# Values put off by a step, Strassen's form in all but three first layers, gates broadcast by DMA

## The chip, the cores and the metric

The kernel runs on one core of a Trainium2 chip. The metric is the time of one execution on the device in microseconds, the median of four runs. The profile is that of one execution.

## The reference

The input x has 8 images of 256 channels and 32 x 32 pixels (1024 tokens each). All is float32. Two layers follow one another:

- Layer 0: group normalisation; queries by a 1x1 convolution; keys and values by another one, then pooled to four sizes (32, 16, 11 and 5 squared, 1426 places), each with a 3x3 depthwise convolution added and a layer normalisation; attention with 8 heads of 32 channels; a small mixing matrix between channels; a projection, added to x.
- Layer 1, on tokens: layer normalisation, attention with one head of 256 channels over 1024 tokens, added. Then layer normalisation and a mixture of 8 experts, added. The experts are where part of the change lies:

```
feat = mean(x, axis=0);  w = softmax(feat @ Wr + br)      # gates, by token place and expert
h = relu(bn(x @ W1[e] + b1[e]))                           # first layer, 256 -> 256
h = relu(bn(h @ W2[e] + b2[e]))                           # second layer
y = h @ Wo[e] + bo[e]                                     # third layer
out = sum over e of y * w[:, e]
```

The gates depend on the mean over all 8 images, so they are known only when attention of the last image has ended.

## The kernel before

Channels lie on the 128 partitions (two blocks of 128), tokens along the free axis. TensorE, ScalarE (ACT), VectorE (DVE), GpSimd (POOL) and the transfers of SyncE (SP) run at the same time, each through its own queue, in program order. What the program order is, a planner in the kernel decides while the program is built: the class `Flow` keeps a modelled clock for each engine and for each tile the time at which it will be ready or free. Work is written as generators ("threads") that yield what they need next: an engine, tiles, and a PSUM tag. `Flow.step` runs threads that its model finds runnable. Without an argument it is closed for TensorE and lets only the other engines' work through. With a pair of paces it first adds credit, up to 1.5 times the pace, for threads of rank under 5 and for those of rank 5 and above; TensorE's work of a thread is let in while its class has credit, or while TensorE's clock is earlier than the time at which the score buffer will be free. `Flow.finish` runs threads until a condition holds. All instructions pass through line 668, so the profile's groups are told apart by tile names.

*Stage 1, layer 0's attention with layer 1's attention beside it (0 to about 1990 us).* 384 steps: 8 images, 2 groups of 4 heads, 2 halves of 512 queries, 12 chunks of up to 128 keys. In a step four matmuls (`scores`) fill the tile `sc` (128 x 4 x 512, half of PSUM, one buffer), four heads side by side by rows of the array; ACT takes exp of it into `pt` (six buffers). Then four matmuls (`values`) of the chunk before add into `pv` (one buffer, one bank), side by side by columns. Every two chunks POOL issues a DMA that adds the odd chunk's `pt` onto the even one's (`add`); DVE adds these pairs up to the sum for the softmax (`sums`), and a unit of 12 chunks ends with ACT's copy of `pv`. The work of other threads that fills TensorE between these is called filler here: projections, transposes, normalisations, all of layer 1's attention (`layer1`, `outputs`). It goes through the PSUM tags `sm` (two buffers) and `sx` (one).

The order in a step of the loop at the end of `attention` is: scores of chunk i and their exp, a closed step, values of chunk i - 1, the pair's addition, and a step with the paces 4 and 2 us for filler.

*Stage 2, experts beside the end of layer 1 (about 1990 to 2275 us).* A tile is half an image (512 tokens), item i is one expert on one tile, 128 items. While the thread `gates` is not done, the loop runs first and second layers of the items in turn, each of four matmuls of 512 columns (two instructions each), and lets the planner put the rest of layer 1 and the gates between. Second layers' results (`h2`) are stored to DRAM (`h2d`). At its end `gates` broadcasts each gate row to 128 partitions by a matmul with `sel` and an ACT copy into `gates` (16 times), and makes four tiles of the output's bias.

*Stage 3 (to the end).* Pools of layer 1 are closed and new ones opened. First and third layers go in Strassen's form (the Winograd variant): seven matmuls of 256 columns on combinations of the weights (`weights`, on POOL) and of the input (`combined`, on DVE), and `sums` on DVE and ACT to put the seven products of a first layer together (`first7`). Stored results are fetched (`fetch`), multiplied by their gate and combined (`weigh`), and third layers add up over the eight experts in PSUM (`third`).

Of the kernel before, what the change touches and what calls it, by code (L numbers as in the profile page):

```python
# [13 lines left out]
PSUM = bass.MemoryType.PSUM  # L14
# [20 lines left out]
AHEAD = {"DVE": 4.0, "ACT": 2.0, "POOL": 1.0, "SP": 10.0}  # L35
NEAR = {"DVE": 1.5, "ACT": 2.0, "POOL": 1.0, "SP": 10.0}
BUFS = {"sm": 2, "sx": 1}
PACE2 = 8.0
NBOUND = 64
# [840 lines left out]
def attention(tc, kit, f, outer, ended, nb, consts, x, t1, t2, hn, bounds, vecs, q_t, kv_t, proj_t, gqk_t, wqk, wqkv, vecs1, w1_d, w1c, gate_d, wrc, vecs2, bnvec):  # L880
# [6 lines left out]
    with ExitStack() as ctx:  # L887
# [924 lines left out]

        pts = {}
        for i in range(len(steps) + 1):
            if i < len(steps):
                b, c, half, kc = steps[i]
                sl = slice(half * 512, half * 512 + 512)
                if kc % 4 == 0:
                    f.finish(lambda: key_parts[0] > 3 * b + kc // 4)
                if (half, kc) == (0, 0):  # L1820
                    f.finish(lambda: (b, c) in qs and (b or (c, 0) in asked))
                    turn[0] = 2 * b + c
                    atts[b, c] = T(work, [P, HW], "att", bufs=2)
                if i == 4:
                    f.finish(lambda: {0, 1}.issubset(whole))
                if b == 0 and kc == 0:
                    f.finish(lambda: (c, half) in asked)
                pts[i] = scores(b, c, sl, kc)
                f.step()
            if i:  # L1830
                b1, c1, half1, kc1 = steps[i - 1]
                if kc1 == 0:
                    pv = T(psum, [P, 512], "pv")
                    pairs = []
                    sl1 = slice(half1 * 512, half1 * 512 + 512)
                    f.spawn(unit(b1, c1, sl1, i // NKC, pairs), 0)
                f.finish(lambda: kc1 // 4 in vts[b1])
                values(b1, c1, kc1, pts[i - 1], pv)
                if kc1 % 2:
                    add(kc1, pts.pop(i - 1), pts[i - 2])  # L1840
                    pairs.append(pts.pop(i - 2))
                if kc1 == NKC - 1:
                    f.finish(lambda: projected[0] >= b1)
                    f.act.activation(atts[b1, c1][:, sl1], pv, AF.Copy)
            if i < len(steps):
                f.step((PACE, PACE1))
        f.finish(lambda: projected[0] == nb)
# [139 lines left out]

def experts(tc, kit, nb, t2, hn, h2d, w1c, w2_d, wo_d, bnvec, bo_d, gate_d, wrc, consts8, out, f, outer, ended, early):

# [10 lines left out]
    with ExitStack() as ctx:  # L2000
# [24 lines left out]
        f.sp.dma_start(br, gate_d[:, 2 * NE :])  # L2025
        sel = T(wg, [NE, NE * P], "sel")
        f.sp.dma_start(sel, consts8[:, : NE * P])
        bo = T(wg, [NE, C], "bo")
# [3 lines left out]
        gt = T(wg, [NE, HW], "gt")  # L2032
        gb = T(wp, [P, NE, HW], "gates")
        gated = []

        def gates():


# [36 lines left out]
            for half in range(2):  # L2075
# [5 lines left out]
                f.ve.tensor_copy(gt[:, half * 512 : half * 512 + 512], ps[:NE, :])  # L2081
            for half in range(2):
                sl = slice(half * 512, half * 512 + 512)
                for e in range(NE):
                    yield "PE", (gt,), "sm"
                    ps = T(shared, [P, 512], "sm", bufs=2)
                    f.pe.matmul(ps, lhsT=sel[:, e * P : (e + 1) * P], rhs=gt[:, sl], start=True, stop=True)
                    f.act.activation(gb[:, e, sl], ps, AF.Copy)
            added = T(wp, [P, 2, HW], "featsum")
# [42 lines left out]

        def second(i, staged):
            _, e, _, _ = where(i)
            h, src = T(work, [P, 2, 512], "h2", bufs=5), h1s.pop(i)
            for m in range(2):
                half(h, w2[e], e, src, 2, 3, m)
                yield
            if staged:
                f.sp.dma_start(h2d[i], h)  # L2140
            else:
                h2s[i] = h

        def fetch(i):
            if i not in h2s:
                h = h2s[i] = T(work, [P, 2, 512], "h2", bufs=5)
                f.sp.dma_start(h, h2d[i])

        total = 2 * nb * NE
        f.spawn(gates(), 7)  # L2150
        n1 = n2 = n3 = 0

        while not gated and n2 < NSTAGED:
            first(n1)
            n1 += 1
            f.step((PACE2, PACE2))
            if n1 > 1:
                for _ in second(n2, True):
                    pass
                n2 += 1  # L2160
                f.step((PACE2, PACE2))
        f.finish(lambda: gated)
        early.close()
        wp3 = ctx.enter_context(tc.tile_pool(name="w3", bufs=1, side="right"))
        psum_y = ctx.enter_context(tc.tile_pool(name="psum_y", bufs=1, space=PSUM, side="right"))

        def blocks(w):

            return w[:, 0, :P], w[:, 1, :P], w[:, 1, P:]

        def weights(w, tag):
            s = T(wp3, [P, 4, P], tag)
            a11, a12, a22 = blocks(w)
# [5 lines left out]

        def combined(h, tag):  # L2180

            t = T(wp3, [P, 4, C], tag, bufs=2)
            f.ve.tensor_tensor(t[:, 0:2, :], h[:, :, C:], h[:, 0, :].rearrange("p (n q) -> p n q", n=2), ALU.subtract)
            f.ve.tensor_tensor(t[:, 2, :], h[:, 1, C:], t[:, 0, :], ALU.subtract)
            f.ve.tensor_tensor(t[:, 3, :], h[:, 1, :C], t[:, 2, :], ALU.subtract)
            return t
# [22 lines left out]
        def sums(banks):  # L2209

            c = T(wp3, [P, 4, C], "c", bufs=2)
            u = T(wp3, [P, 2, C], "u", bufs=2)
            p26, p57, p34 = (banks[i].rearrange("p (u q) -> p u q", u=2) for i in (0, 2, 3))
            p1 = T(wp3, [P, 1, C], "p1c", bufs=2)
            f.act.activation(p1[:, 0, :], banks[1][:, :C], AF.Copy)
# [6 lines left out]
        def first7(i):  # L2222
# [10 lines left out]
            if e == NE - 2 and tile_i + 1 in xs:  # L2233
                ts[tile_i + 1] = combined(xs[tile_i + 1], "t1")

        def weigh(i):
            _, e, _, sl = where(i)
            h = h2s[i]
            f.ve.tensor_tensor(h, h, gb[:, e : e + 1, sl].to_broadcast([P, 2, 512]), ALU.mult)
            h2s[i] = h, combined(h, "t3")  # L2240

# [14 lines left out]

        s1, s3 = {}, {}
        for i in range(NE):
            s3[i] = weights(wo[i], f"s3e{i}")
            e = (n1 + i) % NE  # L2260
            s1[e] = weights(w1[e], f"s1e{e}")

# [10 lines left out]

        for i in range(2):
            fetch(i)
        weigh(0)
# [19 lines left out]
def tile_conv_attn_hybrid(  # L2296
# [35 lines left out]
    w1c = T(dram, [P, NE, 2, C], "w1c")  # L2332
    wrc = T(dram, [P, 2, NE], "wrc")
    h2d = [T(dram, [P, 2, 512], f"h2_{i}") for i in range(2 * nb * NE)]

# [3 lines left out]
    flag = T(cpool, [P, 1], "flag")  # L2339
    last = partial(experts, tc, kit, nb, t2, hn, h2d, w1c, w2_d, wo_d, bnvec, bo_d, gate_d, wrc, consts8, out)  # L2340
    with ExitStack() as early:
# [132 lines left out]
```

## Time and profile before

| | |
|---|---|
| median of 4 runs (lowest to highest) | 3383.7 us (3379.43 to 3385.47) |
| the profiled execution: time, span | 3385.09 us, 3382.8 us |
| granted TensorE clock, mean | 0.978 |
| TensorE, DVE, ACT, POOL busy | 95%, 67%, 50%, 15% of the span |
| TensorE busy from 0 to 2000 us | 1845 us |
| TensorE busy from 2050 to 2270 us | all of it |

An engine's idle time costs something only where the engine sets the pace. Durations of matmuls are modelled and overlap by their ends, so the distance from one start to the next is the better measure: two instructions of 512 columns start 0.43 us apart, of 256 columns 0.22 us. A matmul in float32 is two instructions. A wait is given as engine and tile that waited, what released it, and the time in total, the number of waits and the longest.

### The profile page before, as it was taken

Reading aid. Unit: us, or ns where it says so; the run is one execution under the profiler, and the core shown is the slowest. Engines: PE = TensorE matmul, PEld = TensorE weight load, DVE = VectorE, ACT = ScalarE, POOL = GpSimd, SP = SyncE. Lnnn points to the kernel's source line nnn. Section 1 sums busy time; section 2 is a strip of 40 time slices with the busy share of each in tenths; the row PEclk is TensorE's granted clock in tenths of the full one; section 3 lists DMA queues with packets and bytes.
Section 4 is the critical chain, followed back from the end, with each engine's and each line's share of the span. In section 5 each row is a group of like instructions: output and inputs, shape, how many; then the busy total and the mean of one; then the engine's idle time right before and its main releaser. Section 6 shows DMA issues by size and latency. Waiting matters only on the chain.

```text
span 3382.8 us, 39921 instructions
## 1 busy us (share of the span) xinstructions
PE 3201.3 (95%) x15270; PEld 1781.6 (53%) x15270; DVE 2266.3 (67%) x3890; ACT 1694.3 (50%) x2222; POOL 519.1 (15%) x644
## 2 busy tenths in 40 slices
PE   8687899899899999899999989999999999999998
PEld 4322245344345345344344446637777777777775
DVE  6687787886986887877875444207766666666665
ACT  4476676576576666666665533342233333333332
POOL 2211414213213214213212110013000000000000
PEclk9798999999999999999999999999999999999999
DMA  2366646646656566556557563213430000000000
GB/s 74 82 128 156 137 93 156 134 98 152 134 127 126 125 149 125 115 129 128 111 118 153 116 204 136 79 72 134 162 106 19 31 26 19 19 19 19 19 13 20
DMA packets 102328, 335.37 MB, mean 99 GB/s; under 512 B 12576, under 2 KB 37928, under 8 KB 78896
## 3 DMA queue, kind: packets, MB, share of 16 engines
q0 software_dynamic: 28608, 179.85, 27.7%
q1 hardware_dynamic: 70160, 150.91, 13.0%
q8 instruction: 122, 2.00, 0.2%
q10 hardware_dynamic: 3360, 1.97, 0.2%
q14 instruction: 78, 0.64, 0.1%
HBM read 97.28 MB, written 70.26 MB: 50 GB/s over the span
## 4 chain that ended last, share of the span: by engine, by line
PE 49%; DVE 1%; ACT 1%; DMA 0%; issue 0%; SPq 0%; DVEq 0%; ACTq 0%
PE bank L668 25%; PE y L668 11%; PE sm L668 7%; PE sc L668 2%; PE sx L668 2%; PE pv L668 2%; ACT pt L668 1%; DVE t L668 0%; DMA h<-h 0%; DMA hn<-hn 0%; DVE h L668 0%; DVE pt L668 0%; DMA t<-pt 0%; DVE rec L668 0%; DVE c L668 0%
## 5 line engine op out<-in xcount | busy, mean ns | idle before, releaser
L668 ACT ACTIVATE pt<-sc 128x2048 f32<-128x2048 f32 (+1 forms) x384 | 719.9, 1875 | 325.7 <-PE sc L668 271.4
L668 DVE SCALAR_TENSOR_TENSOR acc<-p,vec,acc 128x225 f32<-128x225 f32 (+7 forms) x928 | 526.5, 574 | 28.6 <-ACT acc L668 4.1
L668 PE MATMUL sc<-q,kn 32*128 32x512 f32 (+1 forms) x3072 | 448.1, 653 | 93.2 <-ACT pt L668 91.5
L668 DVE TENSOR_TENSOR pt<-pt,pt 128x1024 f32<-128x1024 f32 x320 | 387.3, 1253 | 144.0 <-DMA pt<-pt 134.3
L668 PE MATMUL bank<-h,w2e 128*128 128x512 f32 x1024 | 478.2, 593 | 0.0
L668 ACT ACTIVATE h<-bank,bnvec 128x512 f32<-128x512 f32 x300 | 231.2, 771 | 476.9 <-PE bank L668 456.8
L668 PE MATMUL pv<-pt,vt 128*32 128x512 f32 (+1 forms) x3072 | 422.6, 623 | 0.0
L668 ACT ACTIVATE h<-c,bnvec 128x512 f32<-128x512 f32 x212 | 161.0, 807 | 321.8 <-DVE c L668 321.8
L668 POOL DMA_DIRECT2D pt<-pt x192 | 173.7, 905 | 778.5 <-ACT pt L668 611.3
L668 DVE TENSOR_TENSOR c<-p1c,bank 128x512 f32<-128x512 f32 x106 | 72.8, 687 | 309.2 <-PE bank L668 309.2
L668 PEld LDWEIGHTS bank<-h,w2e 128*128 128x128 f32 x1024 | 193.9, 190 | 151.0 <-issue 139.4
L668 PEld LDWEIGHTS sc<-q,kn 32*128 32x128 f32 (+1 forms) x3072 | 116.6, 179 | 285.4 <-ACT pt L668 185.4
L668 PEld LDWEIGHTS pv<-pt,vt 128*32 128x32 f32 (+1 forms) x3072 | 61.0, 108 | 303.6 <-issue 292.9
L668 POOL TENSOR_TENSOR rstd<-rstd,mhalf 128x4 f32<-128x4 f32 (+2 forms) x88 | 105.7, 1202 | 688.7 <-DVE rstd L668 593.2
L668 DVE TENSOR_TENSOR h<-h,gates 128x1024 f32<-128x1024 f32 x128 | 157.3, 1229 | 71.4 <-DMA h<-h 64.3
L668 PE MATMUL bank<-hn,w1e 128*128 128x256 f32 (+1 forms) x600 | 191.6, 448 | 10.2 <-DMA hn<-hn 10.2
L668 PE MATMUL y<-t,s3e 128*128 128x256 f32 x768 | 188.0, 381 | 0.0
L668 PE MATMUL sm<-y,t 128*128 128x256 f32 x752 | 180.4, 385 | 0.0
L668 PEld LDWEIGHTS sm<-y,t 128*128 128x128 f32 x752 | 137.9, 190 | 56.1 <-issue 34.4
L668 PEld LDWEIGHTS bank<-hn,w1e 128*128 128x128 f32 x600 | 114.4, 192 | 100.2 <-issue 92.7
L668 ACT ACTIVATE p<-sm 128x512 f32<-128x512 f32 (+1 forms) x151 | 88.5, 586 | 146.5 <-PE sm L668 124.6
L668 PE MATMUL bank<-t,s1e 128*128 128x256 f32 x636 | 155.7, 381 | 2.0 <-DVE t L668 2.0
(306 smaller groups left out, 4671.6 us busy)
## 6 DMA issues: line engine op xcount, KB each, us to landing
pt<-pt POOLq DMA_DIRECT2D x160, 1024.0 KB, 7.4
h<-h SPq DMA_DIRECT2D x76, 512.0 KB, 4.2
xi<-in_x_dram SPq DMA_DIRECT2D x16, 512.0 KB, 6.0
t<-t SPq DMA_DIRECT2D x8, 1024.0 KB, 9.3
res<-t SPq DMA_DIRECT2D x32, 256.0 KB, 4.1
t<-res SPq DMA_DIRECT2D x32, 256.0 KB, 5.0
hn<-res SPq DMA_DIRECT2D x32, 256.0 KB, 2.9
hn<-hn SPq DMA_DIRECT2D x16, 512.0 KB, 5.3
```

The costliest lines, as they stand in the source:

```text
L668: ins = fn(*args, **kwargs)
```

## The change

In the attention loop the filler step comes before the values. Values of the chunk before are put off by one step if it is the only one outstanding and the planner's TensorE clock, plus SLACK of 0.5 us, has passed the time at which `sc` will be free. In the next step both chunks' values are issued. After values a step runs with paces of zero, which also cuts the credit that is left over to zero.

In the experts' stage the combined weights of W1 are made by POOL at the start, in the pool where the gates lay; only the first three first layers are plain, all others take `first7`. The thread `gates` writes its 8 x 1024 result to a DRAM tile `gtd`; the 16 sel matmuls and ACT copies go. After the old pools have been closed, 16 DMAs read rows of `gtd` into the 128 partitions of the new tile `gates`, and two more rounds of first and second layer run before the first `weigh`.

```diff
-NEAR = {"DVE": 1.5, "ACT": 2.0, "POOL": 1.0, "SP": 10.0}
+NEAR = {"DVE": 1.5, "ACT": 2.0, "POOL": 1.0, "SP": 1.0}
+SLACK = 0.5
...
                 pts[i] = scores(b, c, sl, kc)
                 f.step()
+            if i < len(steps):
+                f.step((PACE, PACE1))
             if i:
-                b1, c1, half1, kc1 = steps[i - 1]
+                late.append(i - 1)
+            if i < len(steps) and len(late) == 1 and f.now["PE"] + SLACK > f.free("sc"):
+                continue
+            while late:
+                k = late.pop(0)
+                b1, c1, half1, kc1 = steps[k]
...
-                values(b1, c1, kc1, pts[i - 1], pv)
+                values(b1, c1, kc1, pts[k], pv)
                 if kc1 % 2:
-                    add(kc1, pts.pop(i - 1), pts[i - 2])
-                    pairs.append(pts.pop(i - 2))
+                    add(kc1, pts.pop(k), pts[k - 1])
+                    pairs.append(pts.pop(k - 1))
...
             if i < len(steps):
-                f.step((PACE, PACE1))
+                f.step((0, 0))
...
-        sel = T(wg, [NE, NE * P], "sel")
-        f.sp.dma_start(sel, consts8[:, : NE * P])
...
-        gb = T(wp, [P, NE, HW], "gates")
...
-            for half in range(2):
-                sl = slice(half * 512, half * 512 + 512)
-                for e in range(NE):
-                    yield "PE", (gt,), "sm"
-                    ps = T(shared, [P, 512], "sm", bufs=2)
-                    f.pe.matmul(ps, lhsT=sel[:, e * P : (e + 1) * P], rhs=gt[:, sl], start=True, stop=True)
-                    f.act.activation(gb[:, e, sl], ps, AF.Copy)
+            f.sp.dma_start(gtd, gt)
...
+        s1 = {e: weights(w1[e], f"s1e{e}", wp) for e in range(NE)}
+
+        def ahead():
+            nonlocal n1, n2
+
+            (first if n1 < 3 else first7)(n1)
+            if n1 == 0:
+                ts[0] = combined(xs[0], "t1")
+            n1 += 1
+            f.step((PACE2, PACE2))
+            if n1 > 1:
+                for _ in second(n2, True):
+                    pass
+                n2 += 1
+                f.step((PACE2, PACE2))
+
+        f.step((PACE2, PACE2))
+        while not gated and n2 < NSTAGED:
+            ahead()
+        f.finish(lambda: gated)
+        early.close()
+        wp3 = ctx.enter_context(tc.tile_pool(name="w3", bufs=1, side="right"))
+
+        gb = T(wp3, [P, NE, HW], "gates")
+        f.split(gb, *(512 * i for i in range(1, 2 * NE)))
+        for part in range(2):
+            sl = slice(part * 512, part * 512 + 512)
+            for e in range(NE):
+                f.sp.dma_start(gb[:, e, sl], gtd[e : e + 1, sl].to_broadcast([P, 512]))
...
         for i in range(NE):
-            s3[i] = weights(wo[i], f"s3e{i}")
-            e = (n1 + i) % NE
-            s1[e] = weights(w1[e], f"s1e{e}")
+            s3[i] = weights(wo[i], f"s3e{i}", wp3)
...
         for i in range(2):
+            ahead()
             fetch(i)
         weigh(0)
```

The tiles of `combined` and `sums` for first layers move to the pool `work2`; those of third layers stay in `w3`.

## The prediction

> **What bounds the kernel now.** I read the page first, then the waits, then TensorE's timeline at three places, then the chain. The page says that TensorE is busy nearly everywhere:
>
> ```profile
> PE 3201.3 (95%) x15270; PEld 1781.6 (53%) x15270; DVE 2266.3 (67%) x3890; ACT 1694.3 (50%) x2222; POOL 519.1 (15%) x644
> ...
> PE   8687899899899999899999989999999999999998
> ```
>
> So a change is worth what it takes off TensorE's work or idle time, and little else. The third slice (about 85 to 340 us) holds the worst of it; from about 2000 us on only one gap is left. The waits name the idle time:
>
> ```profile
> ACT pt L668 <- PE sc L668: 271.4, 250, 3.9
> ...
> DVE pt L668 <- DMA pt<-pt: 134.3, 59, 8.5
> ...
> PE sc L668 <- ACT pt L668: 91.5, 93, 3.3
> ...
> ACT pt L668 <- DMA pt<-pt: 15.4, 7, 3.5
> ```
>
> The third line is what part one aims at: scores (sc) wait for exp (pt), since sc has one buffer. The fourth is the next limit: exp waits 7 times for a free buffer of pt. Two ways in which a step goes, from the timeline (start, length, instructions, idle time before in brackets):
>
> ```profile
> 893.30 1.14 PE L668 MATMUL sc<-q,kn 32*128 32x512 f32 x8
> 894.37 1.07 PE L668 MATMUL pv<-pt,vt 128*32 128x512 f32 x8
> 896.44 1.14 PE L668 MATMUL sc<-q,kn 32*128 32x512 f32 x8 [1.00 <-ACT pt L668]
> ...
> 1711.28 1.14 PE L668 MATMUL sc<-q,kn 32*128 32x512 f32 x8
> 1712.35 1.06 PE L668 MATMUL pv<-pt,vt 128*32 128x512 f32 x8
> 1713.34 1.99 PE L668 MATMUL sx<-p,v 128*128 128x256 f32 x8
> 1715.27 1.14 PE L668 MATMUL sc<-q,kn 32*128 32x512 f32 x8
> ```
>
> A step without other work lasts 3.14 us, 1.00 of it idle. A full one has scores 1.07, values 0.99 and one filler 1.93, with no wait. The third place is the passage from layer 1 to the last stage:
>
> ```profile
> 2220.83 1.98 PE L668 MATMUL sm<-gt,sel 8*128 8x512 f32 x4
> 2222.74 3.70 PE L668 MATMUL bank<-hn,w1e 128*128 128x512 f32 x8
> 2226.37 1.98 PE L668 MATMUL sm<-gt,sel 8*128 8x512 f32 x4
> ...
> 2272.60 3.70 PE L668 MATMUL bank<-h,w2e 128*128 128x512 f32 x8
> 2284.30 2.04 PE L668 MATMUL y<-h,wo 128*128 128x256 f32 x4 [7.99 <-DVE h L668]
> ```
>
> The gates' broadcast costs TensorE time between expert layers, and the first third layer comes after 7.99 us of idle. Last, the chain, whose pieces give the steady rhythm:
>
> ```profile
> 2334.64 4.74 PE bank L668 x18
> 2347.14 4.74 PE bank L668 x18
> ...
> 2517.38 6.46 PE bank L668 x22
> 2526.86 6.45 PE bank L668 x22
> ```
>
> **The change, part by part**, against the profiled execution: span 3382.8, time 3385.1, which is 1.4 above the median 3383.7.
>
> *First layers.* 300 ACT writes of h from bank by two, less 128 second layers, are 22 plain first layers; 106 are in Strassen's form. After, three stay plain, so 19 change. The rhythm 12.50 holds one third layer more than the rhythm 9.48 (50 instructions against 36), so 14 instructions of 256 columns take 3.02 us. A plain layer takes 3.44 (8 instructions: 2181.52 to 2184.96). 19 x 0.42 = 8 us less on TensorE. Each adds DVE sums (0.69 + 0.69 + 0.42 + 0.68 = 2.5 us) and an ACT copy of 0.38; they lie beside TensorE, in 2000 to 2200 where DVE is 28 to 39% busy. Without this cover they would cost up to 19 x 2.5 = 47 us. All four banks are taken, but second's two are read before the next product needs them: banks 1 and 0 by the sums 0.7 to 2.3 us into the products.
>
> *Weights' sums on POOL.* The 32 for w1 move from 2272 to the start of the stage. At 0.46 us each from the first landing (issued 1994.7, 6.6 to landing) they end at 2016, just when POOL's next work, rstd at 2016.7, stands in the queue behind them. At the contended 0.64 to 1.44 they'd delay layer 1's last norms by about 10 us; TensorE has expert layers to fill that (busy throughout 2050 to 2270). Costed at nothing; if the fill failed, 10 us.
>
> *Gates.* One pair of sel matmuls and the expert half between takes 5.54 us (2220.83 to 2226.37), the half alone 3.44: 2.10 a pair, eight pairs, 17 us less. ACT loses 16 copies of 0.60, off the path. Added: one write of gt and 16 loads of 256 KB on SP. The eight loads of wo took SP 4.92 us, so 16 take 9.8, and what SP has behind them waits: the staged store of h2 and the fetch that the first weigh needs. For the data the nearest rows are the loads of w1e, w2e (256 KB, 6.4 to 6.6 us to landing) at 292 to 393 GB/s: 4.2 MB in some 12 us.
>
> *The passage.* Before: 7.99 idle, then 2.00 for the first t. After: two more rounds of first and second (6.46 each, 12.9 us) cover it; the fetch is issued at about 10, lands at about 16 (5.0 as at 2277.6, and behind the gates), weigh takes 1.5: idle about 5, and the 2.0 goes since ts is there. 5 us less; from 10 less (all hidden) to 10 more (the loads half as fast).
>
> The Trainium skill (DMA: Bandwidth & Descriptors, Rules for kernel authors) speaks against 16 loads of a quarter MiB: it wants a MiB a transfer. By its formula of 2.0 us and the bytes by 436 GB/s each would take 2.6 us, 42 one after another, the fetch would land near 46, and this part would be 25 us worse than I say. The rows above show such loads overlapping, so the sum goes by them.
>
> *Attention.* The order in a step becomes scores, filler, values; values are put off when the filler alone reaches the end of exp as the planner sees it. It plans exp at 1.87 with 0.15 on either side, less SLACK: 1.67 us of filler. I went through TensorE's timeline step by step. 96 of 383 steps end in a wait, 92 us together; 58 have no filler. Applying the rule to the fillers as they lie, 149 steps put off, and 32 of them are followed by a step that waited, where a second set of values (0.86) fills the gap: 22 us less. The other waits lie in runs of empty steps, where nothing is there to move.
> A step of 3.99 has work of its own of 0.86 (eight tiled instructions of 512, four side by side) + 0.86 + 1.72 = 3.44; 0.55 goes into three changes of tiling, 0.18 each. A step put off saves one of the six of two steps: 149 x 0.18 = 27 us less; bounds 0 and 31 (0.21, scores to values).
> Against this: every addition of a pair (POOL's DMA, 7.4 us to landing) is issued after the filler, on average 2.6 us later, and one step more where the odd chunk is put off; pt stays taken. From the starts of exp and the ends of DMAs and sums I get how long a buffer of pt had been free at each exp: under 2.6 us in 5%, under 7 in 30%. With such delays some 50 exps come 1 to 3 us late; where TensorE has filler nothing is lost. I take 15 us more, bounds 0 and 80. DVE's sums, queued with the convolution behind them, wait for the same DMAs (134 us already); the planner plans the landing at 9.7 us, above the measured 7.4, which covers it.
> Last, where chunk 11 is put off (149/383 of 32 units, 12), values of chunk 0 follow at once on the one pv buffer: TensorE waits for ACT's copy (0.60, both signals, at times an exp before it), 1.4 us: 17 more; bounds 10 and 36. The credit that is cut to nothing after values only moves filler; NEAR for SP is read by no thread.
> Attention: -22 - 27 + 15 + 17 = -17, with every term at its end from -22 - 31 + 0 + 10 = -43 to 0 + 0 + 80 + 36 = +116.
>
> **Sum:** -8 - 17 - 5 - 17 = -47: 3385.1 - 47 = 3338; less the 1.4, 3337 against the median.
>
> **Rivals.**
> (a) Attention gives nothing: what the smoother steps save comes back at the places where the loop must finish the next keys, or at pt. For it: the idle windows recur once a batch (1100 to 1200, 1350 to 1400, 1600 to 1650) where DVE is near 90%. Against it: DVE is 75% busy over the stage. Then 3384 - 30 = 3354.
> (b) All of attention's gain and a hidden passage: -43 - 25 - 10 = 3306. For it: pt waits were 15 us only, and the rule sees a late exp and then doesn't put off. Against it: the pv copy is certain.
> (c) Slower: pt's six buffers become the bound. On average 5 are held; 2.6 us more for each pair's two and a step (4.9) for odd put-offs takes that near 6. Then exp waits for the DMA in most steps and TensorE behind it. It decides the sign from 30 us of net loss in attention (0.08 a step); 60 would give 3414. Against it: a late exp leaves TensorE filler in two thirds of the steps.
> (d) The gates' loads are slow or behind others: the passage costs 25 more, 3362.
>
> **How the numbers follow.** Forecast (3320 to 3350) 0.48; (a) 0.15; (b) 0.14; (c) 0.14; (d) 0.05; no change within 0.2% (6.8 us, about what a measurement of this kernel can tell) 0.04. Faster is 0.82, same 0.04, slower 0.14. The range leaves out (c) and some of (b): 3302 to 3386; the forecast's own is 3320 to 3350.
>
> **What would show it.** TensorE's waits of sc for pt near 70 instead of 91.5; pv in groups of 16 instructions in some 150 places; new waits of pv on ACT's copy near 17; exp's waits for DMA pt<-pt grown from 15 to some 50; the end of scores (1966 before) earlier by some 17; no sel; s1e matmuls at 750 instead of 636; one idle stretch near 2230 of 5 us. The prediction falls if scores end later than 1966, if exp waits for pt over 100 us, or if that stretch is over 15.

## The result, and the profile after

The changed kernel takes 3393.3 us (median of 37 runs) against 3383.4 for the kernel before (61 runs): a ratio of 1.0028, interval 1.0022 to 1.0033. It is slower by 0.28%, 10 us; forecast was 47 us less. The profiled execution took 3389.4 us, its span 3387.5, at a mean granted clock of 0.977.

The page's busy times and TensorE's row of slices after the change:

```profile
PE 3175.5 (94%) x15352; PEld 1813.0 (54%) x15352; DVE 2308.9 (68%) x3972; ACT 1682.6 (50%) x2225; POOL 501.0 (15%) x644
...
PE   8687899999999999999989989998999999999998
```

TensorE is busy 26 us less than before (3201.3), and yet the span is longer: 30 us more of idle time (span less busy time: 212.0 against 181.5). So the work was saved, and waits ate it. Stage 1 tells where. This is the view by windows, the stretch from 0 to 1985 us, first of before, then of after; its columns are the length, then the busy time and the instructions of TensorE, its weight loads, DVE, ACT and POOL, then granted clock, DMA share and GB/s:

```profile
0.00:1985.00 1985.00, 1840.42 (x10239) 830.74 (x10240) 1493.64 (x2670) 1242.58 (x1516) 467.33 (x563) 0.97 0.58 125
```

```profile
0.00:1985.00 1985.00, 1811.36 (x10104) 820.98 (x10105) 1479.07 (x2644) 1229.21 (x1499) 457.73 (x561) 0.97 0.57 124
```

Attention's last scores start at 1963.88 us (1965.75 before), but 135 fewer matmul instructions were done by 1985. The loop has a fixed number of steps, so it ends on time whatever is left over; work of layer 1 that didn't get in beside attention runs later.

I went through TensorE's instructions in the trace, each counted once, and split the time from the first scores to the start of the last ones into four: idle time; filler's own work (its columns at 0.214 us per 256); scores and values at 0.86 us a chunk each; and the rest (changes of tiling, slow clock, waits that the modelled ends hide).

| | first to last scores | idle | filler's own work | scores, values | rest | length less filler |
|---|---|---|---|---|---|---|
| before | 1887 | 130 | 917 | 658 | 182 | 970 |
| after | 1886 | 160 | 888 | 657 | 181 | 997 |

The last column is what the loop takes apart from the filler it hides: 27 us more (all numbers are rounded one by one). Of the two terms in which the change was to save, idle time grew by some 30 us and the rest, which holds the changes of tiling, stayed as it was. Waits of before that the readings below rest on, then those of after:

```profile
POOL pt L668 <- ACT pt L668: 611.3, 93, 12.5
...
PEld sc L668 <- ACT pt L668: 185.4, 130, 4.2
```

```profile
ACT pt L669 <- PE sc L669: 320.8, 249, 4.9
POOL pt L669 <- PE pv L669: 318.1, 46, 17.3
PEld sc L669 <- ACT pt L669: 252.5, 190, 5.2
...
DVE pt L669 <- DMA pt<-pt: 161.3, 60, 8.4
...
PE sc L669 <- ACT pt L669: 95.4, 77, 4.3
...
ACT pt L669 <- DMA pt<-pt: 70.1, 23, 5.5
```

Scores wait for exp fewer times (77 against 93) but not for less time (95.4 us against 91.5). Sorted by what held exp up, the waits where exp was on time (it began within 0.2 us of its scores' end) fell from 63.5 to 34.7 us, as forecast; those where exp had itself waited for an addition's DMA rose from 15.4 to 36.8, and those where exp was late for another reason, mostly its place in ACT's queue, from 12.6 to 23.9. Exp's waits for a free pt went from 7 (15.4 us) to 23 (70.1 us). DVE's sums wait 27 us more for the additions.

The second line is new: the additions now stand in POOL's queue until TensorE has done values (318 us). Before, what came last for them was exp (611.3 us). The reason is in what an addition writes. It adds onto the even chunk's tile, so it must wait until the even chunk's values have read that tile; the odd chunk's values it needn't wait for, since both only read. Before, the even chunk's values had ended in all 192 pairs when the odd chunk's exp ended; after, they end later than that exp in 128 of them. From the end of the odd chunk's exp to the issue of the addition it took 0.3 us in the median (1.9 in the mean) before, and 4.8 (5.3) after.

Two put-off steps from TensorE's timeline near the end of the loop:

```profile
1952.70 1.14 PE L669 MATMUL sc<-q,kn 32*128 32x512 f32 x8
1953.77 1.99 PE L669 MATMUL sm<-wv,t 128*128 128x256 f32 x8
1955.84 1.14 PE L669 MATMUL sc<-q,kn 32*128 32x512 f32 x8
1956.91 1.98 PE L669 MATMUL sx<-t,gw 128*128 128x512 f32 x4
1958.83 1.92 PE L669 MATMUL pv<-pt,vt 128*32 128x512 f32 x16
1960.68 1.14 PE L669 MATMUL sc<-q,kn 32*128 32x512 f32 x8
```

The order is as meant: scores and filler, then scores, filler and 16 instructions of values. The first of the two steps lasts 3.14 us (1952.70 to 1955.84) with 0.86 + 1.71 = 2.57 of own work: as long as an empty step of before, since exp sets its end. 131 steps are put off (149 were forecast), and some 35 of them are of this kind. The changes of tiling that fall away there are not won; time for values is gained only in the second step. The wait hardly shows as TensorE's idle time, because the modelled end of the filler reaches up to it; it stands under the weight load of scores (third line of the waits: 252.5 us, 185.4 before).

The passage to the last stage, on TensorE, SP and DVE:

```profile
2312.73 3.60 PE L669 MATMUL bank<-h,w2e 128*128 128x512 f32 x8
2326.23 2.07 PE L669 MATMUL y<-h,wo 128*128 128x256 f32 x4 [9.91 <-DVE h L669]
...
2331.70 1.03 PE L669 MATMUL y<-h,wo 128*128 128x256 f32 x4
```

```profile
2293.59 10.98 SPq L669 DMA_DIRECT2D h<-h  x2
2304.74 12.49 SPq L669 DMA_DIRECT2D gates<-gtd  x16
2317.64 3.51 SPq L669 DMA_DIRECT2D h<-h  x5
```

```profile
2324.95 1.23 DVE L669 TENSOR_TENSOR h<-h,gates 128x1024 f32<-128x1024 f32 x1 [11.14 <-DMA h<-h]
```

The first row is two stores of second layers; SP waits for the second one's result most of the 10.98 us. Then come the 16 gate loads, which hold the queue for 12.49 us. A load with nothing to wait for takes SP 0.32 to 0.45 us; the later ones wait. The chain shows on what (start, length, what ran):

```profile
2305.92 5.67 DMA gates<-gtd
2311.59 0.02 issue
2311.61 7.31 DMA gates<-gtd
```

The load issued at 2305.92 is the third, the one at 2311.61 the eleventh: in this program a transfer of SP goes out only when the one issued eight before it has landed. The third row begins with another store; the fetch for the first weigh is the second in it, goes out at 2318.31 and lands at 2324.73. DVE gets to weigh at 2324.95, and TensorE has waited 9.91 us.

### The profile page after: what moved, and what is told of

It reads as the page before. It is cut to its first block, busy times and chain, and to the rows that moved or that the text cites. A ratio compares the mean times of both kernels' runs of the same rounds, so it can differ in the third digit from the quotient of the medians.

```text
span 3387.5 us, 40258 instructions
## 1 busy us (share of the span) xinstructions
PE 3175.5 (94%) x15352; PEld 1813.0 (54%) x15352; DVE 2308.9 (68%) x3972; ACT 1682.6 (50%) x2225; POOL 501.0 (15%) x644
## 5 line engine op out<-in xcount | busy, mean ns | idle before, releaser
L669 PE MATMUL sc<-q,kn 32*128 32x512 f32 (+1 forms) x3072 | 450.1, 656 | 105.3 <-ACT pt L669 95.4
L669 PE MATMUL pv<-pt,vt 128*32 128x512 f32 (+1 forms) x3072 | 394.1, 612 | 5.3 <-ACT att L669 5.3
L669 ACT ACTIVATE h<-bank,bnvec 128x512 f32<-128x512 f32 x262 | 201.1, 769 | 395.6 <-PE bank L669 376.8
L669 ACT ACTIVATE h<-c,bnvec 128x512 f32<-128x512 f32 x250 | 189.9, 807 | 386.5 <-DVE c L669 386.5
L669 DVE TENSOR_TENSOR c<-p1c,bank 128x512 f32<-128x512 f32 x125 | 85.9, 687 | 353.6 <-PE bank L669 352.7
L669 PEld LDWEIGHTS sc<-q,kn 32*128 32x128 f32 (+1 forms) x3072 | 117.1, 180 | 387.8 <-ACT pt L669 252.5
L669 PE MATMUL sm<-p,v 128*128 128x256 f32 x832 | 194.0, 385 | 1.6 <-ACT sm L669 1.6
L669 PEld LDWEIGHTS pv<-pt,vt 128*32 128x32 f32 (+1 forms) x3072 | 73.5, 109 | 215.0 <-issue 200.1
L669 PE MATMUL bank<-t,s1e 128*128 128x256 f32 x750 | 182.3, 379 | 0.0
L669 PEld LDWEIGHTS sm<-p,v 128*128 128x128 f32 x832 | 156.4, 191 | 47.5 <-issue 22.2
L669 DVE TENSOR_TENSOR h<-h,gates 128x1024 f32<-128x1024 f32 x128 | 156.0, 1218 | 18.3 <-DMA h<-h 11.1
L669 PEld LDWEIGHTS y<-t,s3e 128*128 128x128 f32 x768 | 146.8, 191 | 20.2
```

What stands on the lines that cost most here:

```text
L669: ins = fn(*args, **kwargs)
```

## Experiments

Every ratio is to the kernel before, run beside the variant. Beside each time I give the column "length less filler" from the same count over TensorE's instructions where it tells something; with the old loop it is 970 or 971.

### Which part costs

The experts' part with the loop of before, and the loop of after with the experts' part of before:

```diff
 e1, against after
-            if i < len(steps):
-                f.step((PACE, PACE1))
...
-            if i < len(steps) and len(late) == 1 and f.now["PE"] + SLACK > f.free("sc"):
-                continue
-            while late:
-                k = late.pop(0)
-                b1, c1, half1, kc1 = steps[k]
+                b1, c1, half1, kc1 = steps[i - 1]
...
-                f.step((0, 0))
+                f.step((PACE, PACE1))
 e2, against before: these lines the other way round
```

> The loop of attention is the one of before; the experts' stage is the changed one. Theory A: the experts' part gives what was forecast and attention takes it away again, since in the changed kernel's trace scores end at the same time as before while some 31 us of layer 1's filler are left over for the next stage. Then this kernel takes 3350 to 3360 us. Rival B: the first layers and the transferred gates bring nothing, attention is neutral. Then it takes 3385 to 3395 us.

> The loop of attention is the changed one; the experts' stage is the one of before. Theory A: 3383 plus 30 to 40, 3413 to 3423 us. Rival B: 3380 to 3388 us. If the parts add up, the gains and losses of the two half changes make together the 10 us that the whole change costs.

e1: 3361.0 us, ratio 0.9941 (0.9919 to 0.9963), length less filler 971. e2: 3414.7, 1.0092 (1.0075 to 1.0109), 994. So the experts' part gives 23 us, and the attention loop takes 30. Together they make +7; the whole change measured +10. All that follows on the loop is about these 30 us.

### The cut credit

A step with paces of zero also cuts the credit left over. That could be why filler is left over. In e4 this step neither adds to the credit nor cuts it (keep).

```diff
-                f.step((0, 0))
+                f.step((0, 0), keep=True)
```

> The changed kernel, but the step after the values adds no credit and doesn't cut what is left, so filler with credit runs there too, as before. Theory C: the filler that is left over is work that the cut credit kept out; then 31 us of it return into attention and the kernel takes 3360 to 3372 us. Rival D: the order or the putting off itself loses them (later additions, pt held longer); then it stays within 7 us of 3393.

3419.4 us, 1.0106 (1.0090 to 1.0123), outside both ranges. The filler's own work came back to 925 us (917 in before), but attention's last scores moved to 2018.6 us and idle time was 170 us; length less filler 1016. Credit is not the cause: the loop gets its filler in and is longer for it. Filler left over is the loss showing up, not the loss.

### The additions

If later additions do the harm (theory P), a loop without any should show the gain. In e7 (old loop) and e8 (new loop) the DMA that adds the odd chunk's exp to the even one's is left out; the odd chunks are missing in the softmax's sums.

```diff
         def add(kc, pt, into):
-            w = KEY_CHUNKS[kc][1]
-            f.pool.dma_start(
-                out=into[:w].rearrange("p j q -> p (j q)"), in_=pt[:w].rearrange("p j q -> p (j q)"), accum_op=ALU.add
-            )
+            return
```

> Experts' part as changed, old loop, and the DMA additions of pairs are left out (odd chunks are then missing in the softmax sums). pt comes free right after the values, DVE doesn't wait for DMAs. Theories P and Q both: a little under 3361, 3335 to 3358 us.

> The whole change, and the DMA additions of pairs are left out in the same way. Theory P: the only thing that made the new loop worse is gone; the saved waits remain, so it takes 10 to 30 us less than the old loop without additions. Theory Q: it stays 15 to 35 us slower than the old loop without additions, as with them (32).

e7: 3340.5 us, 0.9870 (0.9854 to 0.9887), length less filler 944. e8: 3320.7, 0.9810 (0.9794 to 0.9827), 916. With the additions the new loop is 32 us slower than the old one (after against e1), without them 20 us faster. TensorE's waits of scores for exp, in e7 and then in e8:

```profile
PE sc L669 <- ACT pt L669: 83.0, 94, 2.6
```

```profile
PE sc L669 <- ACT pt L669: 45.1, 54, 1.7
```

Here the change does what the forecast said it would: 40 fewer waits, 38 us less. It is the additions that turn it round. Theory Q, that filler between scores and values is the cause by itself, had e8 15 to 35 us slower than e7; TensorE's idle time before filler does grow without the additions, but only from 34 to 43 us.

The reverse: the old loop, where only the addition is issued late, after the step's filler instead of ahead of it.

```diff
                 values(b1, c1, kc1, pts[i - 1], pv)
-                if kc1 % 2:
-                    add(kc1, pts.pop(i - 1), pts[i - 2])
-                    pairs.append(pts.pop(i - 2))
...
                 f.step((PACE, PACE1))
+            if i and kc1 % 2:
+                add(kc1, pts.pop(i - 1), pts[i - 2])
+                pairs.append(pts.pop(i - 2))
```

> Old loop and the experts' part; the only edit is that the DMA addition of a pair is issued after the step's filler instead of right after the values, so TensorE's order is meant to stay scores, values, filler. Theory P (late additions are what the new order costs): most of the 24 us by which the order alone is slower than the old loop, 3373 to 3390 us, with exp's waits for additions 40 to 60 us instead of 17. Theory Q (filler between scores and values is the cause): 3356 to 3368 us, as the experts' part alone.

3455.8 us, 1.0211 (1.0193 to 1.0228): 95 us over e1, length less filler 1065. Its waits, where e1 has 95.1 us and 17.4 us on these lines:

```profile
PE sc L669 <- ACT pt L669: 135.3, 113, 7.2
...
ACT pt L669 <- DMA pt<-pt: 126.4, 39, 8.2
```

So a later place of the addition in the program, with scores, values and filler in their old order, brings a loss with the same mark, exp waiting for the DMA that frees pt. Its size doesn't follow from the delay alone. From the odd chunk's exp to the addition's issue it is 1.0 us in the median and 3.8 in the mean (0.3 and 1.9 in e1): many additions go out as before, and more of them stand behind other work in POOL's queue (96 go out more than 1 us after exp, 71 in e1). e5 below has the same mean delay and loses 24 us. The planner also orders other work anew when the addition moves; what part of the 95 us comes from that is open.

### What of the additions: pt's buffers or DVE's queue

An addition that lands late holds pt's buffers, which delays exp, and holds up DVE's sums, with all that is queued behind them. A seventh buffer might tell these apart; it wasn't tried. Instead DVE's wait is taken away: each of its sums adds the first pair to itself and reads no other pair, so the softmax's sums are others.

```diff
-                    yield ve(s, pairs[i])
-                    f.ve.tensor_tensor(s, s, pairs[i][:, j : j + 2, :], ALU.add)
+                    yield ve(s)
+                    f.ve.tensor_tensor(s, s, s, ALU.add)
```

> Old loop and the experts' part; DVE's sums add the first pair to itself and don't read the other pairs (so the softmax sums are others): as many DVE instructions, none waits for an addition, and a buffer of pt is held until the addition has landed, no longer until DVE has read it. Theory V (VectorE's queue): less than 3361, 3340 to 3355. Theory P (buffers of pt): the same direction, as pt is held 3 us less.

> The whole change with the same sums. Theory V: the loss is gone, it takes 10 to 25 us less than the old loop with such sums. Theory P: exp still waits for additions 40 us or more and it stays 10 to 30 us slower than the old loop with such sums.

e13 (old loop): 3361.2 us, 0.9918 (0.9902 to 0.9935), as e1. e14 (new loop): 3378.0, 0.9974 (0.9963 to 0.9984). The gap between the loops is 17 us instead of 32. In e14 DVE waits for the additions only once (1.6 us), but exp still does:

```profile
ACT pt L669 <- DMA pt<-pt: 81.2, 25, 6.7
```

In e13 it is 6 times, 18.3 us. So a loss stays, with exp's waits, when DVE's are gone. That the 15 us between the two gaps are DVE's share is not shown: it is less than the runs with other paces below let one tell. Both theories had e13 faster than e1, and it isn't.

### The order, and the putting off

Three kernels between the two loops. e5 has the new order and never puts off; e6 puts off even chunks only, with whose values no addition is issued; e10 puts off even chunks only and, in steps with an odd chunk, issues the values and the addition right behind the scores, with the filler after them. The last column is the mean time from the end of the odd chunk's exp to the issue of the addition.

```diff
 e5
-SLACK = 0.5
+SLACK = -1e9
 e6
-            if i < len(steps) and len(late) == 1 and f.now["PE"] + SLACK > f.free("sc"):
+            if i < len(steps) and len(late) == 1 and late[0] % 2 == 0 and f.now["PE"] + SLACK > f.free("sc"):
 e10
+            odd = bool(late) and late[-1] % 2 == 1
-            if i < len(steps):
+            if i < len(steps) and not odd:
                 f.step((PACE, PACE1))
-            if i < len(steps) and len(late) == 1 and f.now["PE"] + SLACK > f.free("sc"):
+            if i < len(steps) and not odd and len(late) == 1 and f.now["PE"] + SLACK > f.free("sc"):
                 continue
...
-                f.step((0, 0))
+                f.step((PACE, PACE1) if odd else (0, 0))
```

> The changed kernel, but values are never put off: filler goes ahead of the values in every step, and the credit left over is cut. To be compared with 3361 us (the experts' part alone, old loop) and 3393 (the whole change). Theory P (pt is held longer: additions issued late, most of all those put off by a step): the order alone delays an addition by the filler only, 2.6 us on average; 3365 to 3378 us, and exp waits for the additions 25 to 45 us in all (17 in the old loop, 70 in the new one). Theory Q (filler that stands between scores and values exposes TensorE to whatever that filler waits for): the order alone carries the loss, 3385 to 3400 us.

> The changed kernel, but only the even chunk of a pair may be put off, so that no addition is put off by a step. Theory P: exp's waits for the additions fall from 70 us to 25 to 45, and the time to 3365 to 3380 us. Theory Q: it stays within 7 us of 3393 or of the run without any putting off, whichever order costs.

> The changed kernel, but an odd chunk's values come right after the scores, as in the old loop, with the filler behind them and the addition issued at once; only even chunks have the filler ahead of them and may be put off. Theory P: the additions are no later than in the old loop and part of the waits on exp goes, so 5 to 20 us less than the experts' part alone, 3341 to 3356 us. Theory Q: half of the steps have the costly order, 3370 to 3380 us.

| | us | ratio | length less filler | idle | of it before filler | exp waits for DMA | addition issued after exp |
|---|---|---|---|---|---|---|---|
| e1, old loop | 3361.0 | 0.9941 (0.9919 to 0.9963) | 971 | 132 | 36 | 17.4 us, 9 times | 1.9 us |
| e5 | 3384.7 | 1.0005 (0.9994 to 1.0016) | 986 | 145 | 50 | 57.0 us, 19 times | 3.9 us |
| e6 | 3387.0 | 1.0009 (0.9997 to 1.0020) | 992 | 158 | 54 | 49.9 us, 16 times | 5.5 us |
| e10 | 3397.2 | 1.0042 (1.0026 to 1.0059) | 1000 | 158 | 63 | 36.7 us, 11 times | 3.6 us |
| after | 3393.3 | 1.0028 (1.0022 to 1.0033) | 997 | 160 | 49 | 70.1 us, 23 times | 5.3 us |

The order alone, filler ahead of values and addition, costs 24 us of the 32 without a single put-off, about the least that can be told apart here (see the next section), and exp already waits for the additions 19 times. What the putting off adds to that is too little to tell. e5 and e6 are above what theory P (late additions) had for them, in time and in exp's waits; e5 is at the lower edge of what theory Q had, e6 within it.

e6 and e10 were meant to keep the additions early, and didn't: both put off the even chunk, on whose values the addition waits. In e6 it goes out no earlier than in after. e10 is a miss too: I had forecast 3341 to 3356, since there no addition waits for filler. But the even chunk's values end after the odd chunk's exp in 134 of its 192 pairs, and POOL waits for them as in after:

```profile
POOL pt L669 <- PE pv L669: 345.4, 52, 13.3
```

So e10 is no test of early additions. Exp's waits for the DMA did fall to half of after's, but TensorE's idle time didn't fall: more of it stands before filler (63 us, 27 more than in e1), beside DVE's waits, which were longer than in any other kernel:

```profile
DVE pt L669 <- DMA pt<-pt: 180.5, 72, 7.9
...
ACT pt L669 <- DMA pt<-pt: 36.7, 11, 5.8
```

That filler waits on work behind DVE's sums fits these numbers and was not tested. Why DVE waits longest here stays open.

### More and less filler

The planner hands out filler by two paces, 4.0 and 2.0 us a step. If the loss comes from filler that stands ahead of the additions, smaller paces should shrink the gap between the loops, larger ones widen it. Theory L is the rival that the constants fit the old loop, and any other order is worse by chance. e15 (old loop) and e16 (new loop) have 4.4 and 2.2, as below; e17 and e18 have 3.6 and 1.8.

```diff
-PACE = 4.0
-PACE1 = 2.0
+PACE = 4.4
+PACE1 = 2.2
```

> Old loop and the experts' part, the paces of filler at 4.4 and 2.2 instead of 4.0 and 2.0. Theory L (the constants fit the old loop, and any other order is worse by chance): 15 to 40 us more than 3361. Theories V and P: within 12 us of 3361.

> The whole change with the paces 4.4 and 2.2. Theory L: it moves by 15 to 40 us to either side of 3393. Theories V and P: within 12 us of 3393, still at least 20 slower than the old loop with the same paces.

> Old loop and the experts' part, paces 3.6 and 1.8. If lateness by filler is the cause this says nothing for the old loop, where additions come ahead of filler: within 15 us of 3361. Theory L: 15 to 30 us more, as at 4.4 and 2.2 (26).

> The whole change with paces 3.6 and 1.8. If lateness by filler is the cause: exp's waits for additions fall below 60 us (70 at 4.0) and the gap to the old loop at the same paces below 20 us (32 at 4.0, 25 at 4.4). If the gap has other causes or is a matter of chance, it stays between 20 and 40 or scatters without exp's waits following it.

| paces | old loop | new loop | gap | exp waits for DMA, old and new |
|---|---|---|---|---|
| 4.4 and 2.2 | 3387.4, 1.0004 (0.9994 to 1.0013) | 3412.0, 1.0071 (1.0054 to 1.0088) | 25 | 18.2 and 67.7 us |
| 4.0 and 2.0 | 3361.0, 0.9941 (0.9919 to 0.9963) | 3393.3, 1.0028 (1.0022 to 1.0033) | 32 | 17.4 and 70.1 us |
| 3.6 and 1.8 | 3373.6, 0.9971 (0.9960 to 0.9982) | 3432.0, 1.0145 (1.0128 to 1.0162) | 58 | 33.6 and 99.0 us |

The gap went the other way: with less filler it nearly doubles, so the forecast by the amount of filler falls. What goes with the gap is again exp's wait for the additions: in the new loop with small paces

```profile
ACT pt L669 <- DMA pt<-pt: 99.0, 28, 8.9
```

and idle time in the loop is 188 us against 136 in the old loop, 52 of the 58. Why less filler makes exp wait longer isn't settled: the additions go out 5.4 us after exp in the mean, as in after (5.3).

These four runs also show how finely loops can be compared. These paces shift the whole order, and moved the old loop by 13 and 26 us, at 4.4 and 2.2 as far as theory L had it. Differences between loops under some 25 us (e5 against e1, e6 or e10; 32 against 17 above) are not to be read one by one. The 52 us between the two comparisons with and without additions, and the 95 us of e9, are well beyond it. Chance alone is also hard to square with a new loop that is slower at all three paces.

### The passage

e3 is e1 with the first two fetches issued ahead of the gates, and the gates in two loads of 2 MB; e11 has, beside that, three rounds of expert layers there (range(3) in the last loop below).

```diff
+        for i in range(2):
+            fetch(i)
         for part in range(2):
             sl = slice(part * 512, part * 512 + 512)
-            for e in range(NE):
-                f.sp.dma_start(gb[:, e, sl], gtd[e : e + 1, sl].to_broadcast([P, 512]))
+            f.sp.dma_start(gb[:, :, sl], gtd[None, :, sl].to_broadcast([P, NE, 512]))
...
         for i in range(2):
             ahead()
-            fetch(i)
```

> As the kernel with the experts' part alone, but the fetches of the first two stored items are issued before the gates' loads, and the gates come in two DMAs of 2 MB instead of 16 of 256 KB. Theory: the 9.91 us of idle before the first third layer come from SP's queue, where 16 issues (12.5 us) stand ahead of the fetch. Then the gap closes and with it the slow clock behind it: 10 to 13 us less than the experts' part alone. Rival: the gap comes from the transfers themselves (two of 2 MB need as long as 16 small ones, some 12 us): at most 4 us less.

> As the run with early fetches and two transfers for the gates (3355 us), with three rounds of first and second layers instead of two ahead of the first weigh. In that run 5.3 us of idle were left there, which one more round of 6.5 us covers: 3347 to 3352 us. If the third round only moves the wait on, 3355.

e3: 3355.3 us, 0.9914 (0.9897 to 0.9930). e11: 3351.1, 0.9915 (0.9897 to 0.9933). The idle time before the first third layers, in e1, e3 and e11:

```profile
PE y L669 <- DVE h L669: 11.7, 1, 11.7
```

```profile
PE y L669 <- DVE h L669: 5.3, 2, 2.7
```

```profile
PE y L669 <- DVE h L669: 0.8, 1, 0.8
```

SP's queue in e3, where the two large loads take 1.05 us instead of the 12.49 of the 16 in after:

```profile
2257.36 1.05 SPq L669 DMA_DIRECT2D gates<-gtd  x2
```

11 us of idle time are gone. The time fell by 6 (e3, where 10 to 13 were expected) and 10 us (e11) in the medians; the intervals of e1 and e11 meet, so the sign of that gain is likely rather than certain. e11 is 0.85% faster than before and 1.2% than after: it is the change without its attention loop.

e3 makes two changes at once, and which of them helped was not tested. What is left of its wait ends with the gates: the first large load lands 11.5 us after its issue (2257.36 to 2268.84), and weigh begins at 2269.01. In e1 the first of the small loads, the only one that the first weigh needs, landed after 4.9. So the place of the fetches ahead of the gates may be all of the gain.

> The loop of the mixed run with the passage of three rounds. If the parts add up, the mixed run less 8 to 14 us: by theory P 3330 to 3345 us; by theory Q 3356 to 3370.

e12, e10 with e11's passage: 3384.4 us, 1.0008 (0.9998 to 1.0017), 13 us less than e10, where the passage gave 10 with the old loop. The two parts add up as far as can be told.

## Why the prediction was wrong

Its terms, against the runs:

| term | predicted | measured |
|---|---|---|
| first layers, gates (without the passage) | -8 - 17 = -25 | -26 or -27 (e1's -23, less the passage); TensorE's busy time -26 |
| passage | -5 | +2 to +4 (idle 9.91 and 11.7 against 7.99) |
| waits of scores saved | -22 | -29, where exp was on time |
| changes of tiling | -27 | nothing in the sum: "rest" 182 to 181 |
| pt held longer | +15 | +21 through the DMA, +11 where exp was late otherwise, +12 before filler |
| values waiting for the copy of pv | +17 | +5.3 |

**First layers and gates** were right, as a sum; they weren't tested apart. 750 instructions with the sums of w1 run as forecast, no matmul with sel is left, and DVE's and POOL's added work cost nothing that shows.

**The passage** failed by SP's queue. I had the 16 loads take SP 9.8 us and the fetch go out at about 10; it went out 13.6 us after the first load (2304.74 to 2318.31), since a load waits until the one eight before it has landed, and it landed after 6.4 us where I had 5.0. These 5 us are what the idle time of 9.91 has over my 5. The rows of w1e and w2e gave the loads' own landing rightly (6.7 us median). The Trainium skill (DMA: Bandwidth & Descriptors, Rules for kernel authors) asks for 1 MiB or more a transfer. The formula that I took from the same page, by which this part would have been 25 us worse, is fitted there to transfers that GpSimd issues; these go out on SP. The loads overlapped (4.5 to 8.6 us to landing, 16 of them issued within 12.49), so a sum of one after another was too high. Whether larger loads help is not shown, since e3 also moves the fetches.

**Waits of scores** with exp on time went as the step-by-step reading said. Their total, which was to be near 70 us, came to 95.4, because of the late exps.

**The tiling term** was a mean applied where it doesn't hold. A put-off step without idle time costs 0.43 us over its own work in the median and others 0.56, so 0.13 is saved where I had 0.18; but a step with one filler of 1.71 is set by exp (3.14), and there nothing is saved. The rule picks steps with just enough filler to reach exp's end, so many of them lie on that floor. The sum over the stage didn't fall. I had put the bounds of this term at 0 and 31 and taken 27; the row of the empty step, 3.14, was on the page and spoke for the low end.

**The term that failed most** is "I take 15 us more, bounds 0 and 80", for buffers of pt that are held longer. I counted exps that come late and let TensorE's filler cover most. Exp waited for the DMA 23 times and 70 us, where I said some 50; but by the count TensorE lost more than to those waits: other exps come late too (+11), and it waits longer before filler (+12). That these two follow from the late additions fits, and was not shown one by one. For DVE I wrote that the planner's 9.7 us for the landing "covers it"; DVE's waits rose from 134 to 161 us. In after the issue itself stands behind TensorE's values, as the 318 us in POOL's queue show: the additions go out 3.4 us later after exp in the mean, where I had 2.6 and a step more for some. With terms as measured, -29 for waits, nothing for tiling, +21 + 11 + 12 for exp and filler, +5 for values: +20, where the count has +27 and e2 +30. The rest is not put down to a term.

So the mechanism of rival (c), pt's buffers held by the additions, is the one that the runs point to, at its lower end: it "decides the sign from 30 us of net loss in attention", and the loss was 30 (e2), though exp waited for the DMA in 23 of 384 steps and not in most. I gave it 0.14, on the ground that a late exp leaves TensorE filler. It does; but the time is gone all the same, and 29 us of filler were left to run after the loop.

None of the three signs by which the prediction was to fall came: scores ended before 1966, exp waited under 100 us, the gap was under 15. The signs were badly chosen. The end of scores can't show a loss in a loop that hides other work, since what it loses is the work it no longer hides; the length less the filler done is the sign to look at.

**Shown:** the experts' part gains and the loop loses (e1, e2); the additions decide (e7 and e8; e9 in its direction), and the new order holds them behind the even chunk's values (the trace). **Not settled:** how the loss divides between pt's buffers, DVE and ACT; why e9 loses 95 us; what early additions with the new order would give, since e10 didn't have them; why less filler widens the gap.

## What to carry to other kernels

Before work is moved ahead of a step, list everything the step issues, and ask who waits for the last of it: here the values could wait, but the DMA that adds onto the tile they read had to wait with them, and it frees the buffers on which the very wait that was to be filled depends. Where a loop hides other work, measure its length less the work hidden, not its end. A saving by step is worth nothing in steps whose length another engine sets.

## What the runs showed of the hardware

- What stands ahead of a transfer on the queue of its issuing engine can delay it more than its own bytes. 16 broadcast loads of 256 KB held SP for 12.49 us. A load with no wait took 0.32 to 0.45 us there; the rest is waiting for the landing of the transfer issued eight before, which is how this program uses its semaphores. Two loads of 2 MB took 1.05 together, but the first landed only after 11.5 us, against 4.5 to 8.6 for the small ones.
- After 9.91 us of idle time TensorE ran at half the granted clock for some 4.8 us: the window 2326.20 to 2328.10 has 0.50, and the four instructions at 2326.23 took 2.07 us where the same four at 2331.70 took 1.03. The Trainium skill (TensorE: Matmul & The Clock Gate, Part 1) says that the clock halves after an idle window of some 3.4 us; this agrees with it. So the gap cost its own length and, by an estimate, about 2.4 us more (half of the 4.8).
- An accumulating DMA of 1 MB within on-chip memory took 7.5 us from issue to landing (median of 160), and one of 144 KB 4.5 (32 of them). Issued 0.3 us after the odd chunk's exp (median, e1), these DMAs made exp wait 17 us in all; issued 4.8 us after it (after), 70 us.
